# Pair 2's transposes and their copies, emitted with its normalising and ahead of pair 0's products

## The chip, the cores and the metric

The kernel runs on one core of a Trainium2 chip. Times are device microseconds (us) of one execution. A time quoted for a kernel is the median of its runs; every run of this study was of the fast state. Engines are named as in the profile: PE is TensorE, ACT ScalarE, DVE VectorE, POOL GpSimd, and SP the engine whose queue starts the transfers. L311 is line 311 of the kernel.

## The reference, cut to what matters

Four layers work on `x` of 32 batches x 512 tokens x 128 features. Only the first layer matters here:

```python
h = jnp.maximum(_layernorm(x, axis=-1), 0.0)
x = x + _L0_gnn_ref(h, adj, W, e, bias)

def _L0_gnn_ref(input, adj, W, e, bias):
    h0 = jnp.einsum('bnf,fg->bng', input, W[0])
    h1 = jnp.einsum('bnf,fg->bng', input, W[1])
    A = ...                       # softmax over the nonzero entries of adj, 512 x 512
    M = jnp.eye(adj.shape[0])
    out = jnp.einsum('ij,bjg->big', A * M, h0) + jnp.einsum('ij,bjg->big', A * (1.0 - M), h1)
    return out + bias[None, None, :]
```

## The kernel before

The 32 batches are 16 pairs. For each pair ACT normalises eight tiles (`normed`, L216). The result is turned feature-major: on PE for pairs 0 to 2, with ACT copying out of PSUM (L240, L243), and for pairs 3 to 15 by DVE's block transposes and a trip through DRAM (L250, L254, L257). PE then projects it (`p_g`, L357). In the next turn of the loop PE multiplies by the attention matrix: seven products by Strassen's scheme and the diagonal (L311, L654), whose evictions on DVE go through a chain of sums `u`, with GpSimd adding to `x`.

```python
def stats_steps(q, hold=False):
    ...                                   # DVE, L194: bn_stats of x
    yield
    nc.scalar.activation(sd, st[:, :, :, 2], AF.Sqrt, bias=eps, scale=1.0 / D)        # L200
    yield
    nc.vector.reciprocal(rs, sd)                                                     # L203
    nc.vector.scalar_tensor_tensor(sh, st[:, :, :, 1], -1.0, rs, OP.mult, OP.mult)   # L205

def pe_steps(h, name, hT):
    ps = [bank(f"p_{name}_{b}") for b in range(2)]
    for b in range(2):
        for t in range(NT):
            nc.tensor.transpose(ps[b][:, blk(t)], h[:, b, t, :], ident)              # L240
    yield
    for b, p in enumerate(ps):
        nc.scalar.copy(hT[:, :, b, :].rearrange(...), crossed(p))                    # L243

def transposed(h, name):
    for b in range(2):
        nc.vector.transpose(hb[:, :, b]..., h[:, b]...)                              # L250
    ...                                   # SP, L254: four writes to DRAM; L257: one load back
    return hT

def layer0_first(q):
    if q >= 4:
        ln_stats(q)
        yield
    h = normed(q)
    yield
    hT = (transposed_by_pe if q < EARLY else transposed)(h, f"hT0_{q}")              # EARLY = 3
    yield
    if q >= EARLY:
        yield
    for _ in project_steps(q, hT):        # PE L357, then ACT's copies g (L389)
        pass

ORDER = ((1, "a", True), (6, "c", True), (5, "d", True), (7, "c", False), (2, "a", False),
         (4, "c", False), (3, "d", False))

def layer0(q):
    ...                                   # GpSimd: hd (L633), x + bias (L645), right blocks (L282 to L285)
    def evict(k, p):
        if k == 1:
            nc.vector.tensor_add(u[:, 0], pv, spread(b0, 2))                         # L663
            nc.gpsimd.tensor_add(x_of(1, 0), x_of(1, 0), u[:, 0])
        elif k == 6:
            nc.vector.tensor_add(u[:, 1], pv, u[:, 0])                               # L666
            nc.gpsimd.tensor_add(x_of(0, 1), x_of(0, 1), u[:, 1])
        elif k == 5:
            held["d"] = pv
        elif k == 7:
            nc.vector.tensor_add(u[:, 2], pv, u[:, 0])                               # L671
            nc.vector.tensor_add(u[:, 2], held["d"], u[:, 2])                        # L672
            nc.gpsimd.tensor_add(x_of(1, 1), x_of(1, 1), u[:, 2])
        ...                               # k = 2, 4, 3, and the last diagonal: L676, L679, L682, L688
```

`late_sums` makes eight additions of 128x512 on GpSimd for the second layer, one in each turn of the loop from turn 3 on (L275). The schedule puts generators into turns:

```python
waiting = [[layer0(q)] for q in range(NQ)]
next(waiting[0][0])
next(first[2])                            # pair 2's normalising
next(first[3])
next(first[3])                            # pair 3's normalising and block transposes
...
waiting[0] += [first[2], first[4]]
waiting[1] += [first[3], first[5]]
for q in range(6, NQ):
    waiting[q - 4].append(first[q])
waiting[3].append(late_sums())
```

The framework's scheduler then settles each engine's issue order by what it takes to be ready; the source order is a priority only. `keep_in_program_order` and `issue_after` pin an instruction behind another of its engine.

Of the kernel before, what the change touches and what calls it, by code (L numbers as in the profile page):

```python
# [24 lines left out]
def kernel(  # L25
# [345 lines left out]
# [6 lines that stand above are left out]
        hT = (transposed_by_pe if q < EARLY else transposed)(h, f"hT0_{q}")  # L377
# [3 lines that stand above are left out]
        for _ in project_steps(q, hT):  # L381
            pass
# [28 lines left out]
    first = {q: layer0_first(q) for q in range(2, NQ)}  # L411
# [224 lines left out]
    def loads(q):  # L636
        for b in (2 * q, 2 * q + 1):
            tc.keep_in_program_order(load_x(b))
        yield
# [172 lines left out]
    waiting = [[layer0(q)] for q in range(NQ)]  # L812
    next(waiting[0][0])
    next(first[2])
    next(first[3])
    next(first[3])
    for q in range(NQ // 2, NQ):
        waiting[q - NQ // 2].append(loads(q))
    waiting[0] += [first[2], first[4]]
    waiting[1] += [first[3], first[5]]  # L820
    for q in range(6, NQ):
        waiting[q - 4].append(first[q])
    waiting[3].append(late_sums())
# [46 lines left out]
```

## Time and profile before

| | before |
|---|---|
| median of the first 3 runs | 990.46 us |
| profiled run: span, mean granted PE clock | 988.6 us, 0.996 |
| PE busy | 970.4 us, 98% |
| pair 2's projection begins | 60.78 us |
| then each pair takes, in steady state | 9.83 us |

Read it so: PE works without a gap nearly everywhere, so a pair takes its 9.83 us of PE work, 8.04 for the products and 1.79 for a projection. The start of each pair's projection on PE is therefore a ruler: a step longer than 9.83 us is time lost in that pair. The engines' busy time, from the page:

```profile
PE 970.4 (98%) x5918; PEld 805.4 (81%) x5918; DVE 590.4 (60%) x1392; ACT 469.3 (47%) x1063; POOL 399.3 (40%) x526
```

The averages hide stages. This is the windows view of the kernel before (length, then busy us and instructions of PE, PEld, DVE, ACT and POOL; then clock, DMA share, GB/s):

```profile
80.00:90.00 10.00, 10.00 (x92) 10.00 (x91) 8.00 (x24) 4.64 (x12) 9.43 (x12) 1.00 0.58 161
90.00:100.00 10.00, 9.61 (x86) 9.42 (x85) 8.15 (x20) 4.41 (x12) 9.92 (x13) 1.00 0.59 157
```

GpSimd, 40% busy over the kernel, is 99% busy from 90 to 100. PE waits 0.39 us there, and the step from pair 5 to pair 6 is 0.65 us over 9.83. The prediction below does not look at this stretch.

### The profile page before, as it was taken

What the parts mean: (1) busy time and instruction counts of PE and PEld (TensorE: products, weight loads), DVE (VectorE), ACT (ScalarE), POOL (GpSimd) and SP (SyncE); (2) the same over time, 40 slices, a digit from 0 to 9 for tenths busy, and PEclk for the clock granted to TensorE, in tenths of its full rate; (3) what the DMA queues carried; (4) which work ended last, traced back from release to release, by engine and by line L of the source; (5) the groups of instructions that cost most, each with busy time, mean ns of one, the idle gap of its engine ahead of it and who ended that gap; (6) DMA issues with size and microseconds to landing.
All of it is one profiled execution on the core that took longest, in us unless ns stands there. A gap on an engine that the chain in (4) does not pass through costs nothing.

```text
span 988.6 us, 16123 instructions
## 1 busy us (share of the span) xinstructions
PE 970.4 (98%) x5918; PEld 805.4 (81%) x5918; DVE 590.4 (60%) x1392; ACT 469.3 (47%) x1063; POOL 399.3 (40%) x526
## 2 busy tenths in 40 slices
PE   8979999999999999999999999999999999999998
PEld 4679999999999999999977887777767776777776
DVE  8667878656556565566567666665655444444444
ACT  4845455303232232336767654554574554445553
POOL 2559998752134421311243344444133322233322
PEclk9989999999999999999999999999999999999999
DMA  9264544512213122135423343223132121121111
GB/s 257 84 177 129 155 146 109 148 44 60 70 43 86 44 64 65 46 87 145 108 73 115 117 123 106 71 79 87 45 88 77 48 75 54 54 75 44 54 33 43
DMA packets 83023, 87.17 MB, mean 88 GB/s; under 512 B 6784, under 2 KB 73088, under 8 KB 82944
## 3 DMA queue, kind: packets, MB, share of 16 engines
q1 hardware_dynamic: 82944, 86.14, 30.6%
q8 instruction: 47, 0.77, 0.3%
q14 instruction: 32, 0.26, 0.1%
HBM read 44.70 MB, written 41.42 MB: 87 GB/s over the span
## 4 chain that ended last, share of the span: by engine, by line
PE 91%; ACT 1%; DVE 1%; POOL 1%; issue 0%; DVEq 0%; ACTq 0%
PE p_av L780 12%; PE p_l L357 11%; PE p_score L767 11%; PE p_msgT_c L304 4%; PE p_x2T_c L304 4%; PE p_x1T_c L304 4%; PE p_l_c L311 4%; PE p_feat L357 3%; PE p_msgT_d L304 3%; PE p_x1T_a L304 3%; PE p_hv L357 3%; PE p_x2T_d L304 3%; PE p_x2T_a L304 3%; PE p_x1T_d L304 3%; PE p_msgT_a L304 3%; PE p_qkh L754 3%
## 5 line engine op out<-in xcount | busy, mean ns | idle before, releaser
L216 ACT ACTIVATE h<-x,sh,rs 128x128 f32<-128x128 f32 x512 | 208.7, 483 | 70.3 <-PE p_x2T_d L304 46.5
L772 POOL TENSOR_TENSOR ex<-ex,adjTx 128x512 f32<-128x512 f32 x64 | 83.3, 1303 | 197.1 <-issue 147.7
L768 ACT ACTIVATE ex<-p_score 128x512 f32<-128x512 f32 x128 | 71.6, 588 | 122.8 <-issue 113.0
L780 PEld LDWEIGHTS p_av<-qkh_hv,ex 128*128 128x128 f32 x1024 | 118.4, 191 | 9.6 <-issue 7.2
L780 PE MATMUL p_av<-qkh_hv,ex 128*128 128x129 f32 x1024 | 120.3, 275 | 0.9 <-POOL qkh_hv L761 0.6
L767 PE MATMUL p_score<-qkh_hv,hT 128*128 128x512 f32 x256 | 115.2, 593 | 0.0
L250 DVE STREAM_TRANSPOSE hb_hT<-h 128x512 f32<-128x512 f32 x122 | 84.7, 701 | 27.1 <-ACT h L216 26.3
L194 DVE BATCH_NORM_STATS2 bn<-x 128x6 f32<-128x256 f32 x256 | 95.5, 419 | 2.1
L772 DVE TENSOR_TENSOR ex<-ex,adjTx 128x512 f32<-128x512 f32 x64 | 45.9, 717 | 76.2 <-ACT ex L770 76.2
L767 PEld LDWEIGHTS p_score<-qkh_hv,hT 128*128 128x128 f32 x256 | 46.2, 190 | 46.5 <-issue 44.9
L770 ACT ACTIVATE ex<-ex 128x512 f32<-128x512 f32 x128 | 76.6, 631 | 1.8
L282 POOL TENSOR_TENSOR rt_h<-h 128x256 f32<-128x256 f32 x16 | 11.6, 726 | 133.9 <-PE p_x2T_c L304 133.1
L282 POOL TENSOR_TENSOR rt_feat<-feat,feat 128x256 f32<-128x256 f32 x16 | 11.6, 727 | 128.1 <-ACT feat L723 128.1
L389 ACT COPY g<-p_g 128x512 f32<-128x512 f32 x32 | 18.3, 578 | 67.7 <-PE p_g L357 67.5
L357 PE MATMUL p_l<-th,x1T 128*128 128x128 f32 x256 | 49.5, 275 | 0.0
L357 PE MATMUL p_l<-th,x2T 128*128 128x128 f32 x256 | 49.5, 275 | 0.0
L357 PE MATMUL p_l<-th,hs 128*128 128x128 f32 x256 | 49.5, 275 | 0.0
L357 PEld LDWEIGHTS p_hv<-vw,hT 128*128 128x128 f32 x256 | 33.6, 192 | 15.3 <-issue 8.1
L732 POOL TENSOR_TENSOR x<-x,phi2b 128x256 f32<-128x256 f32 x64 | 44.4, 726 | 0.0
L633 POOL TENSOR_TENSOR hd<-hT,adiag 128x512 f32<-128x512 f32 x32 | 40.4, 1273 | 5.6 <-PE p_l_e L654 3.1
L631 POOL COPY hs<-hT 128x512 f32<-128x512 f32 x32 | 19.6, 611 | 54.7 <-PE p_l L357 40.5
L330 ACT COPY x1T<-p_x1T_a 128x256 f32<-128x256 f32 x16 | 6.0, 372 | 74.8 <-PE p_x1T_a L304 74.8
(227 smaller groups left out, 2144.0 us busy)
## 6 DMA issues: line engine op xcount, KB each, us to landing
d_hT<-hb_hT SPq DMA_DIRECT2D x244, 128.0 KB
hT<-d_hT SPq DMA_DIRECT2D x61, 512.0 KB
x<-in_x_dram SPq DMA_DIRECT2D x32, 256.0 KB
out_dram<-x SPq DMA_DIRECT2D x31, 256.0 KB
adj_s<-in_adj_dram SPq DMA_DIRECT2D x4, 256.0 KB
adjT_d<-adjT SPq DMA_DIRECT2D x1, 1024.0 KB
sq<-in_adj_dram SPq DMA_DIRECT2D x4, 256.0 KB
adjTx<-adjT_d SPq DMA_DIRECT2D x4, 256.0 KB
```

The lines of the kernel that those rows point to most:

```text
L194: ins = nc.vector.bn_stats(st[:, k].rearrange("p e s -> p (e s)"), xt[q][:, b, t : t + 2, :].rearrange("p t f -> p f t"))
L216: nc.scalar.activation(h[:, b, t, :], xt[q][:, b, t, :], AF.Relu, bias=shift[q][:, i : i + 1], scale=scale[q][:, i : i + 1])
L250: nc.vector.transpose(hb[:, :, b].rearrange("p j t r -> p t j r"), h[:, b].rearrange("p t (j c) -> p t j c", c=QR))
L304: nc.tensor.matmul(p[:, :H], b[:, k, :], a[:, k, :], start=(first and k == 0), stop=(k == 1), skip_group_check=True)
L357: nc.tensor.matmul(p[:, blk(t)], hT(t), w, start=(i == 0), stop=(i == len(terms) - 1))
L633: nc.gpsimd.tensor_mul(split(s), src, split(scale))
L732: tc.keep_in_program_order(nc.gpsimd.tensor_add(xi, xi, spread(phi2b, 2)))
L767: nc.tensor.matmul(ps, hT[:, t, b, :], qkh, start=True, stop=True)
L768: nc.scalar.activation(ex[:, t, :], ps, AF.Tanh, scale=1.0 / (8.0 * math.sqrt(D)))
L770: nc.scalar.activation(ex[:, t, :], ex[:, t, :], AF.Exp, scale=8.0)
L772: eng.tensor_mul(ex[:, t, :], ex[:, t, :], adjTx[0][:, t, :])
L780: nc.tensor.matmul(po[:, i, : D + 1], ex[:, t, blk(i0 + i)], hv[:, t, :], start=(t == 0), stop=(t == NT - 1))
```

## The change

The intent: PE stood 6.11 us for ACT's copies of pair 2's transposes, which were issued behind pair 4's normalising. Emitting the transposes and the copies early lets the copies run while PE multiplies pair 0.

```diff
     next(waiting[0][0])
     next(first[2])
+    next(first[2])
     next(first[3])
     next(first[3])
 ...
-    waiting[0] += [first[2], first[4]]
-    waiting[1] += [first[3], first[5]]
+    waiting[0].append(first[4])
+    waiting[1] += [first[2], first[3], first[5]]
```

## The prediction

> **What bounds the kernel now.** I read the page first. TensorE (PE) is busy 970.4 of the 988.6 us of the profiled run, and the chain that ended last is 91% PE. So the kernel gets shorter only where PE stands idle, or where PE works slowly, and both are rare. I then asked the list of waits for PE alone, over the whole run; its columns are: who waited for whom, us in total, times, longest.
>
> ```profile
> PE p_g L357 <- ACT hT L243: 6.6, 2, 6.1
> PE p_adjT L395 <- DMA adj_s<-in_adj_dram: 4.2, 2, 3.5
> PE p_msgT_c L304 <- POOL rt_feat L283: 1.4, 1, 1.4
> PE p_l_c L311 <- DVE u_l L666: 1.2, 2, 0.8
> ```
>
> One wait of 6.1 us stands out, and it is the one that the change aims at: PE waits for ScalarE's (ACT) copies of pair 2's transposes out of PSUM before it can project pair 2. The PE rows of the timeline (start, duration) show where it lies, and what comes after it.
>
> ```profile
> 45.60 1.05 PE L311 MATMUL p_l_a<-g,attT 128*128 128x128 f32 x8
> ...
> 53.64 1.04 PE L240 MATMUL p_hT<-ident,h 128*128 128x128 f32 x8
> 60.78 3.78 PE L357 MATMUL p_g<-w,hT 128*128 128x128 f32 x16 [6.11 <-ACT hT L243]
> ```
>
> The chain that ended last, in order of time, has the same work with its share of the path:
>
> ```profile
> 60.78 3.78 PE p_g L357 x16
> 64.56 1.71 PE p_l_a L311 x8
> 66.27 0.90 PE p_l_c L311 x8
> 73.42 1.79 PE p_g L357 x16
> ```
>
> The reader is to see three things. PE runs without a gap from 45.60 to 54.67. It then does nothing until 60.78. And the first work after the gap is slow: 16 matmuls of a projection take 3.78 us there and 1.79 us one pair later; the next eight take 1.71 instead of 0.89 us. The windows view says why: its last three figures are granted PE clock, DMA share and GB/s.
>
> ```profile
> 54.70:60.80 6.10, 0.02 (x1) 0.02 (x1) 4.18 (x15) 4.53 (x13) 1.24 (x2) 0.88 0.72 223
> 60.80:66.10 5.30, 5.30 (x25) 5.30 (x26) 1.68 (x5) 4.51 (x11) 1.43 (x3) 0.50 0.71 195
> 66.10:73.30 7.20, 7.20 (x66) 7.20 (x66) 4.63 (x13) 0.00 (x0) 5.43 (x8) 1.00 0.81 221
> ```
>
> Last, ACT's rows say why the copies are late, though the transposes were done at 54.7:
>
> ```profile
> 46.73 5.10 ACT L216 ACTIVATE h<-x,sh,rs 128x128 f32<-128x128 f32 x13
> 55.23 0.30 ACT L200 ACTIVATE sd<-bn,eps 128x8 f32<-128x8 f32 x1 [3.40 <-DVE bn L194]
> 55.89 0.30 ACT L200 ACTIVATE sd<-bn,eps 128x8 f32<-128x8 f32 x1 [0.35 <-DVE bn L194]
> 56.88 3.19 ACT L216 ACTIVATE h<-x,sh,rs 128x128 f32<-128x128 f32 x8 [0.68 <-DVE sh L205]
> 59.98 0.29 ACT L200 ACTIVATE sd<-bn,eps 128x8 f32<-128x8 f32 x1
> 60.17 1.04 ACT L243 COPY hT<-p_hT 128x512 f32<-128x512 f32 x2
> ```
>
> The two copies stand in ACT's order behind two square roots, pair 4's whole normalising (8 instructions) and a third square root, which wait in turn for VectorE's (DVE) statistics. ACT itself was idle for 3.40 us before that. In the source the copies come before pair 4's normalising; so the issue order is the framework's scheduler's, which orders by what it believes to be ready, and the source order is only a preference. That matters below.
>
> **What the Trainium skill says.** "TensorE: Matmul & The Clock Gate", Part 1: an idle window of about 3.4 us halves PE's clock, and about 3.4 us of sustained work restores it. The trace agrees in kind: after 6.11 us without work the clock is 0.50, and it is back at 1.00 from about 66; here the slow stretch lasts 5.2 us, longer than the page's figure. Part 4 of that page gives a PE transpose about 275 ns in a kernel; the trace has 272 to 273 ns each, and eight in 1.04 us because they overlap. "DVE: scalar operands, raw-bit mode, write accounting and state across instructions", section 5, says that DVE's queue is one in-order queue. I use it for DVE and assume the same of ACT; that the ready copies above waited behind pair 4 agrees.
>
> **The change, part by part.** It adds and removes no instruction. (1) Pair 2's eight transposes and two copies move in the source from behind pair 0's products to just behind pair 2's normalising, ahead of pair 3's normalising and of the products. (2) Pair 2's projection is moved one list later; it still runs in the step after pair 0's products, only behind pair 4's normalising and pair 1's preparation.
>
> What is removed: the idle time of 60.78 - 54.67 = 6.11 us. With the copies issued behind pair 2's normalising (over at about 48.7, from the 13 above at 0.39 us each, of which 5 are pair 2's) they end near 50.5, long before PE's products end. And with no gap the clock stays up. The slow stretch costs now: projection, from its start to the next group's, 64.36 - 60.78 = 3.58 us against 1.79, so 1.79; the next eight matmuls 66.06 - 64.36 = 1.70 against 0.89, so 0.81; the next 0.04. In all 2.64 us. So the most that can be won is 6.11 + 2.64 = 8.75 us, 0.88% of the time. Everything later is PE's chain, with 3.4 us of PE waits from 90 us on, so what is won here reaches the end.
>
> What is moved onto the path: eight transposes, 0.9 us of PE work. They are only displaced, from behind the products to before or among them; no cost by themselves. But they need pair 2's normalised tiles, which ACT delivers one each 0.4 us from 45.5 to 48.7, while PE could start the products at 45.60. If the transposes are strewn among the products as tiles come ready, PE loses some tenths (I take 0.4). If all eight stand ahead of the products, the last waits until about 48.8, products start at 49.0 and not at 45.6 + 0.9 = 46.5: a loss of 2.5. ACT's copies push pair 3's normalising back by 1.04 us; its transposes go through DRAM and are needed about 11 us later than pair 2's, so that is hidden.
>
> **Rivals.** (a) *The wait only moves to DVE.* Pair 1's products need DVE's evictions: the fourth group reads what the second eviction wrote (the 0.8 us wait in the list above). Before the change DVE does pair 4's and pair 5's block transposes ahead of pair 1's first eviction, and those wait for ACT's normalising. PE would now begin pair 2's projection at about 54.7 plus any stall, pair 1's products 1.8 later, and want the second eviction 4.5 after the start, at about 59.2; pair 4's normalising, started 3.1 us after PE's products end as now, delivers its last tile at about 61, DVE's transpose and two evictions make it 62.7. That would be a new wait of 3.5 us, or about 7 if pair 5's stand ahead as well. Against it: one pair later, where no gap exists, the order is the good one:
>
> ```profile
> 76.14 0.42 DVE L663 TENSOR_TENSOR u_l<-p_l_a,b 128x256 f32<-128x256 f32 x1 [0.37 <-PE p_l_a L311]
> 77.03 0.42 DVE L666 TENSOR_TENSOR u_l<-p_l_c,u_l 128x256 f32<-128x256 f32 x1 [0.47 <-PE p_l_c L311]
> 77.48 0.71 DVE L250 STREAM_TRANSPOSE hb_hT<-h 128x512 f32<-128x512 f32 x1
> ```
>
> Without the gap the first step should look like this one. I give rival (a) 0.3; the time would then be 985 to 989.
> (b) *Transposes as a block ahead of the products*: 8.75 - 2.5 = 6.2 won, 984.2. Source order speaks for it; against it speaks that the scheduler goes by readiness (it put an eviction between pair 2's third and fourth tile without a wait). 0.25.
> (c) *The next transfer becomes the wait.* Pair 3's transposed tiles are fetched back from 56.47 on, and would be wanted at about 54.7 + 1.8 + 8.9 = 65.4. That leaves 9 us, less 1 for the delay on ACT: small, 0.05.
> (d) *The whole gain*, with the strewn order: 8.75 less some tenths, about 8: 982.4. The rest of the chance.
>
> **Range and chances.** Weighing 982.4 (0.4), 984.2 (0.25) and 985 to 989 (0.35), I predict 983.3 us, 7.2 less than 990.46. The range 981.4 to 987.8 leaves out the worst of rival (a) below, and above only what 8.75 and a run's spread of 0.4 us allow. 2% would be 19.8 us, over twice what there is to win, and I see no path to a loss of that size: faster by over 2% 0.01, within 2% 0.98, slower by over 2% 0.01.
>
> **What would show each step.** Right: no wait of PE for the copies; clock 1.00 from 45 to 75; the 16 matmuls of pair 2's projection in 1.8 to 1.95 us, beginning within 2 us of 54.7; a DVE order of both evictions before pair 4's block transposes; the end of the span earlier by just what was won by 75 us. Wrong: a wait of PE on the normalised tiles near 46 to 49 (rival b), or on the second eviction near 60 (rival a), or a clock that drops all the same. The prediction would also fail if the scheduler, given another source order, rearranged later layers; then the difference would grow or shrink after 75 us.

## The result, and the profile after

The changed kernel took 986.01 us (985.0 to 986.21, 4 runs), the kernel before 990.09 (988.56 to 990.57, 4 runs, same chip). The ratio is 0.9959, 95% interval 0.9942 to 0.9977: 4.1 us faster, and the same within 2%. A ratio is the mean time of one kernel's fast runs over the mean of the other's of the same rounds, so it is not quite the ratio of the medians. The profiled span fell from 988.6 to 984.4 us, by 4.2.

PE's waits in the changed kernel (who for whom, us in total, times, longest):

```profile
PE p_adjT L395 <- DMA adj_s<-in_adj_dram: 4.4, 2, 3.7
PE p_l_c L311 <- DVE u_l L666: 1.8, 3, 0.8
...
PE p_l_c L311 <- DVE u_l L671: 1.4, 1, 1.4
...
PE p_hT L240 <- ACT h L216: 0.5, 1, 0.5
```

The wait of 6.1 us for the copies is gone. Three small ones are new. The same windows as in the prediction, in the changed kernel:

```profile
54.70:60.80 6.10, 6.10 (x57) 6.10 (x56) 5.97 (x20) 2.38 (x7) 4.29 (x5) 1.00 0.68 189
60.80:66.10 5.30, 5.28 (x48) 5.09 (x47) 4.49 (x11) 3.75 (x11) 4.16 (x7) 1.00 0.78 208
66.10:73.30 7.20, 6.86 (x62) 6.67 (x61) 5.81 (x19) 6.17 (x16) 6.28 (x8) 1.00 0.52 111
```

The window's last three figures are again granted clock, DMA share and GB/s. PE is full where it was empty, and the clock stays at 1.00 where it was 0.50. So both parts of the 8.75 us were removed. The ruler shows where half of it went. Starts of the projections, in us:

| kernel | pair 2 | pair 3 | pair 4 | pair 5 | pair 6 | pair 10 |
|---|---|---|---|---|---|---|
| before | 60.78 | 73.26 | 83.08 | 92.91 | 103.39 | 142.70 |
| after | 56.41 | 66.52 | 76.95 | 88.44 | 99.16 | 138.47 |
| before: step from the pair left of it | | 12.48 | 9.82 | 9.83 | 10.48 | |
| after: step | | 10.11 | 10.43 | 11.49 | 10.72 | |

From pair 6 on the distance between the kernels is constant, 4.2 us, to the end of the span. The book-keeping: 8.75 us to be won, less 0.26 (the first PE work of this stage began at 45.86 after a longer wait at start-up, for 45.60), less 1.48 (from there to pair 2's projection it took 10.55 us, where the kernel before needed 54.67 - 45.60 = 9.07 for the same work), less 0.28, 0.60, 1.66 and 0.24 in the four steps (each against 9.83; the last against 10.48, which the kernel before had itself). That leaves 4.23, the distance at pair 10.

The 1.48 us, in PE's rows of the changed kernel (start, duration):

```profile
45.86 1.10 PE L240 MATMUL p_hT<-ident,h 128*128 128x128 f32 x3
47.49 0.71 PE L240 MATMUL p_hT<-ident,h 128*128 128x128 f32 x2 [0.54 <-ACT h L216]
48.04 0.61 PE L311 MATMUL p_l_a<-g,attT 128*128 128x128 f32 x4
48.49 0.27 PE L240 MATMUL p_hT<-ident,h 128*128 128x128 f32 x1
...
56.41 1.84 PE L357 MATMUL p_g<-w,hT 128*128 128x128 f32 x15
```

Five of the eight transposes stand ahead of the first product. They follow ACT's tiles one by one and take until 48.04, 2.18 us for 0.55 us of work, so 1.63 us are lost; the other three are strewn among the first product's matmuls. (The book-keeping has 1.48, as the 9.07 us of the kernel before run to the modelled end of its last transpose, 54.67; at the transposes' spacing of 0.11 us a next matmul could have started some 0.15 us earlier.) The later steps: these are all of PE's waits between 57 and 101 us that the view names. A start that came 0.19 us late at 61.06 is below what it names.

```profile
71.49 1.16 PE L311 MATMUL p_l_c<-rt_g,attT 128*128 128x128 f32 x8 [0.34 <-DVE u_l L666]
...
85.21 1.16 PE L311 MATMUL p_l_c<-rt_g,attT 128*128 128x128 f32 x8 [1.40 <-DVE u_l L671]
...
93.70 1.16 PE L311 MATMUL p_l_c<-rt_g,attT 128*128 128x128 f32 x8 [0.63 <-DVE u_l L666]
```

And what DVE did ahead of the eviction at 84.77, for which PE waited 1.40 us:

```profile
81.64 0.71 DVE L250 STREAM_TRANSPOSE hb_hT<-h 128x512 f32<-128x512 f32 x1 [0.49 <-ACT h L216]
84.13 0.71 DVE L250 STREAM_TRANSPOSE hb_hT<-h 128x512 f32<-128x512 f32 x1 [1.79 <-ACT h L216]
84.77 0.39 DVE L671 TENSOR_TENSOR u_l<-p_l_c,u_l 128x256 f32<-128x256 f32 x1
```

The block transposes of pair 7 stand ahead of pair 3's third eviction and wait for ACT's tiles. The eviction's own input had been there since about 82.4 (pair 4's projection at 76.95, 1.79 for it and four groups of 0.89 each).

### The profile page after: what moved, and what is told of

Same layout as the page of the kernel before. It is cut to its first block, busy times and chain, and to the rows that moved or that the text cites. A ratio compares the mean times of both kernels' runs of the same rounds, so it can differ in the third digit from the quotient of the medians.

```text
span 984.4 us, 16128 instructions
## 1 busy us (share of the span) xinstructions
PE 969.2 (98%) x5918; PEld 802.8 (82%) x5918; DVE 590.4 (60%) x1392; ACT 469.6 (48%) x1063; POOL 399.4 (41%) x526
## 4 chain that ended last, share of the span: by engine, by line
PE 88%; DVE 2%; ACT 1%; POOL 1%; DMA 0%; issue 0%; DVEq 0%; SPq 0%; ACTq 0%
PE p_av L780 12%; PE p_l L357 11%; PE p_score L767 11%; PE p_msgT_c L304 4%; PE p_x2T_c L304 4%; PE p_x1T_c L304 4%; PE p_l_c L311 3%; PE p_feat L357 3%; PE p_msgT_d L304 3%; PE p_x1T_a L304 3%; PE p_x2T_d L304 3%; PE p_x1T_d L304 3%; PE p_x2T_a L304 3%; PE p_hv L357 3%; PE p_msgT_a L304 3%; PE p_qkh L754 3%
## 5 line engine op out<-in xcount | busy, mean ns | idle before, releaser
L282 POOL TENSOR_TENSOR rt_h<-h 128x256 f32<-128x256 f32 x16 | 11.6, 726 | 133.9 <-PE p_x2T_c L304 133.1
L282 POOL TENSOR_TENSOR rt_feat<-feat,feat 128x256 f32<-128x256 f32 x16 | 11.6, 727 | 128.1 <-ACT feat L723 128.1
```

## The experiments

Twelve runs were made, one of them the changed kernel again, all correct. Each was timed in the rounds of its batch beside the kernel before. I started with two theories. **Theory 1**: PE's later waits come from block transposes that stand ahead of evictions in DVE's queue while ACT has not yet normalised their tiles; put them behind, and the gain grows. **Theory 2**: the other engines set when pair 6 can begin, near 99 us, whatever PE's own order; take one wait away, and another takes its place. The runs' results, with the starts of the projections:

| run | pair 2 | pair 3 | pair 4 | pair 5 | pair 6 | pair 10 | median, us | ratio to before, 95% |
|---|---|---|---|---|---|---|---|---|
| a_again | 55.53 | 65.64 | 76.07 | 87.57 | 98.31 | 137.61 | 985.65 | 0.9960, 0.9947 to 0.9972 |
| a_dve | 57.15 | 67.25 | 80.02 | 91.55 | 101.38 | 143.18 | 990.74 | 1.0008, 1.0002 to 1.0015 |
| a_both | 54.44 | 65.13 | 76.68 | 86.51 | 100.04 | 140.49 | 989.06 | 0.9993, 0.9985 to 1.0002 |
| c_clock | 65.83 | 75.65 | 85.48 | 95.31 | 105.80 | 145.10 | 992.46 | 1.0024, 1.0015 to 1.0033 |
| a_hb7 | 56.37 | 66.48 | 76.90 | 86.73 | 98.79 | 138.10 | 985.93 | 0.9959, 0.9947 to 0.9972 |
| a_mid | 53.80 | 69.17 | 79.00 | 88.83 | 99.32 | 138.63 | 987.85 | 0.9979, 0.9969 to 0.9989 |
| b_pin | 56.31 | 70.40 | 80.22 | 90.05 | 100.52 | 139.82 | 986.52 | 0.9962, 0.9950 to 0.9975 |
| a_block | 57.62 | 67.45 | 77.60 | 89.11 | 99.07 | 138.38 | 988.19 | 0.9974, 0.9963 to 0.9986 |
| a_hb7s | 56.30 | 66.41 | 76.83 | 86.65 | 96.95 | 136.97 | 983.79 | 0.9940, 0.9927 to 0.9952 |
| a_sums | 55.86 | 65.96 | 76.40 | 87.90 | 97.73 | 137.73 | 985.54 | 0.9955, 0.9942 to 0.9967 |
| b_sums | 59.67 | 70.99 | 80.82 | 90.65 | 100.47 | 140.47 | 989.75 | 0.9999, 0.9991 to 1.0008 |
| a_best | 54.77 | 65.47 | 77.56 | 87.38 | 97.21 | 137.21 | 984.95 | 0.9952, 0.9938 to 0.9965 |

The kernel before had medians of 990.05, 989.9, 989.78 and 990.01 us in the four batches.

### a_again: the changed kernel once more

No edit; it is the common base of the first batch.

> The changed kernel once more, so that the other runs of this call can be compared with it on one chip. Both theories: 0.996 of the kernel before, about 986.0 us, pair 2's projection beginning near 56.4 us, pair 6's near 99.2.

Its steps are those of the first run to 0.02 us; only the start differs, by 0.88 us, as PE's first work of this stage began that much earlier. So the steps belong to the kernel, and nearly a microsecond of the position is chance.

### c_clock: the gap filled with unread matmuls

```diff
 # before.py, in pe_steps, behind the transposes, for pair 2 only
+            for i in range(48):
+                nc.tensor.matmul(idle[:, blk(i % NT)], ident, h[:, 1, i % NT, :], start=True, stop=True, ...)
```

> The kernel before, with 48 matmuls that nobody reads issued behind pair 2's transposes, so that PE has work while it waits for the copies. The clock theory: granted clock stays 1.00, pair 2's projection begins near 60.8 us still, takes 1.8 us and not 3.6, and pair 1's first product group 0.9 and not 1.7; 1.2 to 2.6 us faster than before, 987.5 to 989 us (less than 2.6 if VectorE's evictions, which stand behind pair 5's block transposes, are not ready that early). If the slow matmuls there have another cause (the DMA traffic of that stretch), the projection takes 3.6 us still and the time is 990 us.

PE's rows of the run:

```profile
55.11 10.88 PE L244 MATMUL p_idle<-h,ident 128*128 128x128 f32 x96
65.83 1.95 PE L362 MATMUL p_g<-w,hT 128*128 128x128 f32 x16
```

The filler was nearly twice as long as the gap: 48 float32 matmuls are 96 records of some 0.11 us. So pair 2 began 5.05 us later than in the kernel before, and the run is slower as a whole. What it was made for it shows: with PE kept busy the 16 matmuls of pair 2's projection take their normal time, and the step to pair 3 is 9.82 us, not 12.48. The slow clock was worth 2.66 us in the profile of the kernel before; the prediction had 2.64. The rival on record, DMA traffic, falls too: from 60.8 to 66.1 the DMA share of this run is 0.84 (239 GB/s), more than the 0.71 (195 GB/s) of the kernel before, and the clock there is 1.00 with matmuls at their normal pace. The time, 992.46, is what neither side had expected, because of the filler's length.

### a_dve and a_both: block transposes of pairs 4 to 7 all pinned late

```diff
 # after.py, in transposed, for pairs 4 to 7
-            nc.vector.transpose(hb[...], h[...])
+            tc.keep_in_program_order(nc.vector.transpose(hb[...], h[...]))
 # in layer0: pair q + 3's step is taken behind the fourth product of pair q
-        for _ in products(...): pass
+        for n, _ in enumerate(products(...)):
+            if 1 <= q < 5 and n == 3: next(first[q + 3])
```

a_both also puts pair 2's transposes behind the fourth product group of pair 0, and the copies ahead of the next square root on ACT.

> The changed kernel with VectorE's block transposes of pairs 4 to 7 pinned behind the first four evictions of pairs 1 to 4. Theory 1 (PE's later waits come from block transposes that stand ahead of evictions in VectorE's order and wait for ScalarE): the waits of PE on VectorE from 58 to 99 us, 0.3 + 0.6 + 1.7 + 0.9 us longer than the steady 9.83 us per pair, mostly vanish; pairs follow each other each 9.83 us from pair 3 on; 982.6 to 983.5 us. Theory 2 (the other engines' work sets when pair 6 can start, whatever PE's order): pair 6's projection still begins near 99 us and the time stays at 985.5 to 986.5 us.

> As a_dve, and pair 2's transposes pinned behind the fourth of pair 0's product groups, by when its normalised tiles are all there; the copies come ahead of the square roots on ScalarE. Theory 1: the 1.6 us that PE lost at the head vanish too, pair 2's projection begins near 54.8 us, 981 to 982 us. Theory 2: no more than a_dve, 985.5 to 986.5 us.

Both numbers of both theories missed. SP's queue of a_dve, and the wait that it made on PE:

```profile
66.12 9.12 SPq L256 DMA_DIRECT2D d_hT<-hb_hT  x5
75.47 0.34 SPq L259 DMA_DIRECT2D hT<-d_hT  x1
```

```profile
80.02 2.43 PE L359 MATMUL p_g<-w,hT 128*128 128x128 f32 x16 [2.78 <-DMA hT<-d_hT]
```

Pair 4's load back from DRAM stands in SP's queue behind five writes. The fifth is pair 5's, and pair 5's block transposes had been pinned to 73.61. So pair 4 waited for pair 5's transposes after all, through another queue. The next step, 11.53 us, has no wait of PE at all: the clock was 0.50 from 81.5 to 84.9 (windows view), and half of these 3.4 us is the 1.70 by which the step is too long. These two runs therefore say nothing against Theory 1; they say that the pins were too many. They also put the prediction's rival (c) in its place: in the changed kernel pair 4's load was issued at 71.42. With the 4.55 us that a_dve's load took from issue to PE's start, it would be there near 76.0, an estimate, and pair 4 began at 76.95. It was not the wait, but only 1 us from it.

a_both's head agrees that the 1.48 us are due to the transposes' place: pair 2 began at 54.44. Later on, PE waits 0.60, 1.46 and 0.46 us for DVE's second evictions, and at pair 6 2.82 us for a transfer, as in a_dve. Before the 1.46, DVE had stood 2.31 us for one of GpSimd's additions to x (at 67.71).

### a_mid: transposes among the products, copies early, DVE left to the scheduler

```diff
 # after.py: the second next(first[2]) is taken out, and in layer0(0)
+            if n == 3: next(first[2])     # transposes pinned behind the fourth product on PE,
+                                          # the copies ahead of the next square root on ACT
```

> The changed kernel, with pair 2's eight transposes pinned behind the fourth product group of pair 0 on TensorE and their copies put ahead of the next square root on ScalarE: it keeps the early copies and takes away TensorE's lock-step with ScalarE's normalising. The program's issue order on VectorE comes out differently: halves of the block transposes of pairs 4 to 7 stand before every second eviction of pairs 1 to 3. Theory 1: the head of the changed kernel is 0.7 to 1.6 us shorter (pair 2's projection begins at about 54.8, where the changed kernel had 55.5 and 56.4), but the steps from pair 2 to pair 6 lose more than in the changed kernel, at least 3 us together; time 985.5 to 987.5. Theory 2: pair 6 begins near 99 here too, and the time is 985.7.

Pair 2 began at 53.80, the earliest of all runs. Then PE's rows show the worst step of all:

```profile
57.38 1.06 PE L317 MATMUL p_l_d<-rt_g,sums_att 128*128 128x128 f32 x8
62.28 2.08 PE L317 MATMUL p_l_c<-rt_g,attT 128*128 128x128 f32 x8 [3.85 <-DVE u_l L672]
```

This is the prediction's rival (a), where the prediction put it and nearly of its size (3.5 us): in this order DVE does both halves of pair 4's block transposes before pair 1's second eviction. (L672 of this run is the L666 of the changed kernel.) PE stood 3.85 us, and its clock fell again (0.50 from 61.9 to 65.3, by the windows view); the two together are nearly all of the 5.54 us that the step is too long. The step took 15.37 us. After it PE is so late that nothing else holds it until pair 5, so that pair 6 at 99.32 is no point for Theory 2. The loss in the steps, over 3 us, is as Theory 1 had it; the time, 987.85, is above both theories' numbers. The changed kernel escapes this only because the scheduler set both evictions first there.

### b_pin: the copies alone moved

```diff
 # before.py, in stats_steps
-        nc.scalar.activation(sd, ..., AF.Sqrt, ...)
+        ins = nc.scalar.activation(sd, ..., AF.Sqrt, ...)
+        if q == 4 and q not in early: tc.keep_in_program_order(ins)      # behind pair 2's copies
```

> The kernel before, with only ScalarE's part of the change: its square root for pair 4 is pinned behind pair 2's copies, so the copies stand where the changed kernel has them in ScalarE's queue, while TensorE's transposes stay behind pair 0's products. TensorE should wait about 1.9 us for the copies in place of 6.11 and keep its full clock, so pair 2's projection begins at about 57 and its step to pair 3 is about 10. VectorE's order is the one of the a_mid run. Theory 1: the steps from pair 2 to pair 6 lose at least 3 us together, as there, so the time is 986.5 to 989. Theory 2: pair 6 begins near 99, and the time is 985.7.

PE's rows:

```profile
56.31 2.05 PE L359 MATMUL p_g<-w,hT 128*128 128x128 f32 x16 [1.41 <-ACT hT L245]
...
61.51 0.49 PE L313 MATMUL p_l_a<-g,attT 128*128 128x128 f32 x2 [0.47 <-DVE u_l L665]
63.53 1.71 PE L313 MATMUL p_l_c<-rt_g,attT 128*128 128x128 f32 x8 [1.53 <-DVE u_l L668]
```

With PE's order untouched up to pair 2's projection and only ACT's copies early, the wait for them is 1.41 us, not 6.11, and pair 2 begins as early as in the changed kernel. So the ACT part of the change does the work, and the early transposes on PE are not needed for it. DVE then has the same bad order as in a_mid, and the next step takes 14.09 us, 4.26 too many. Not all of this is DVE: by the windows view the clock is 0.51 from 63.9 to 67.4, after PE waits of only 0.47 and 1.53 us, and half clock for some 3.4 us costs about 1.7 us. The time, 986.52, is at the lower edge of Theory 1's range and above Theory 2's number. Its runs fall into two groups (985.4 to 985.9 with a recorded clock of 1.0, 987.1 to 987.6 with 0.998); the profile is from the slower group. The stretch at half clock is probably what parts them: 3.4 us at half clock lower the mean over 986 us to 0.998 and cost 1.7 us, and the groups' medians lie 1.84 us apart.

### a_block: all eight transposes ahead of the first product

```diff
 # after.py: each of hT0_2's transposes, and pair 0's first product, by keep_in_program_order
```

> The changed kernel, with all eight of pair 2's transposes pinned ahead of pair 0's first product, so that TensorE stands for ScalarE's normalising. The prediction priced this at 2.5 us where the changed kernel showed 1.6 (first product to pair 2's projection against the kernel before). Theory 1: pair 2 begins 0.9 to 1.8 us later than in the changed kernel's two traces (56.4 and 55.5), near 57.3, the later steps are as in the changed kernel (VectorE's order is the same around the evictions), and the time is 986.5 (0.9964). Theory 2: pair 6 begins at the same 98.3 to 99.2, and the time is 985.7.

```profile
47.88 1.86 PE L240 MATMUL p_hT<-ident,h 128*128 128x128 f32 x5 [0.54 <-ACT h L216]
49.58 1.06 PE L315 MATMUL p_l_a<-g,attT 128*128 128x128 f32 x8
```

From the first transpose (46.25) to the first product it took 3.33 us, of which 0.89 is work: a loss of 2.44, as the prediction's rival (b) had it (2.5). But pair 6 begins at 99.07, where the changed kernel had 99.16. The head was 1.2 us worse than in the first run of the changed kernel, and nothing came of it by pair 6: the steps to pairs 3, 4 and 6 were shorter in turn, by 0.28, 0.28 and 0.76 us. That is Theory 2. The medians do not agree with the profile here: three runs are at 985.8 to 986.2 us (the profiled one among them), four at 988.2 to 988.8 with a clock of 0.998. No profile shows the slower group, but 0.998 is what one stretch at half clock of 3.4 us would leave, as in b_pin. That would explain some 1.7 of the 2.65 us between the groups' medians; this is an estimate.

### a_hb7: only pair 7's block transposes moved

```diff
 # after.py, in transposed, for pair 7
+        with tc.issue_after(evicted[name]):            # L672 of pair 3
             nc.vector.transpose(hb[...], h[...])
```

> The changed kernel, with one thing undone on VectorE alone: the two halves of pair 7's block transposes stand behind the third eviction (lines 671 and 672) of pair 3's products, not ahead of it. In the changed kernel VectorE stood 1.79 us at the second half, waiting for ScalarE's normalising, and TensorE then waited 1.40 us for the eviction behind it; the step from pair 4's projection to pair 5's took 11.49 us. Theory 1 (PE's later waits come from block transposes that stand ahead of evictions in VectorE's queue): the 1.40 us wait is gone, that step is about 10.0, and the kernel takes about 1.4 to 1.6 us less than the changed one, 984.1 (0.9940 of the kernel before). Theory 2 (the other engines set when pair 6 can begin, near 99 us, whatever stands first): pair 5 begins earlier, but pair 6 still begins at 98.3 to 99.2 after a new wait, and the time stays at 985.7 (0.9956).

The scheduler also set some of DVE's statistics and one addition to x on GpSimd otherwise. Both theories wrote down what happened first: the wait of 1.40 us is gone, and the step to pair 5 is 9.83 us. Theory 1's time did not come. Pair 6 began at 98.79, and the step to it took 12.06 us in place of 10.72. PE's, DVE's and then GpSimd's rows of this run (seven to nine lines were added above: its L691 is L682 of the changed kernel, its L674 is L667, and its L282 is the L275 of `late_sums`):

```profile
93.16 1.16 PE L318 MATMUL p_l_c<-rt_g,attT 128*128 128x128 f32 x8 [1.80 <-DVE u_l L673]
```

```profile
88.41 0.43 DVE L691 TENSOR_TENSOR x<-p_l_d,x 128x256 f32<-128x256 f32 x1 [1.17 <-POOL x L674]
```

```profile
86.42 1.28 POOL L282 TENSOR_TENSOR adj_s<-adj_s 128x512 f32<-128x512 f32 x1
87.64 0.74 POOL L674 TENSOR_TENSOR x<-x,u_l 128x256 f32<-128x256 f32 x1
```

DVE waited for an addition to x that stood behind an addition of `late_sums`, and PE then waited for DVE. So Theory 2 was right here, and it now had a suspect: GpSimd. I called that **Theory 3**, with the rival **Theory 4** that DVE's own block transposes and statistics of pairs 8 and 9 hold pair 6.

### a_hb7s, a_sums and b_sums: late_sums three turns later

```diff
-    waiting[3].append(late_sums())
+    waiting[6].append(late_sums())
```

This one line was changed in a_hb7, in the changed kernel and in the kernel before. The issue orders of PE, ACT and DVE in the traces are the same, only GpSimd's differs. (The text on record calls the line 282 of the changed kernel; it is 275 there, and 282 in a_hb7.)

> The a_hb7 run, with GpSimd's eight additions of late_sums (line 282 of the changed kernel, 1.28 us each, 10.2 us together) begun three turns of the loop later (turn 6 for turn 3); the issue orders of TensorE, VectorE and ScalarE are the same, only GpSimd's differs. In a_hb7 pair 5 began 1.71 us earlier than in the changed kernel, and pair 6 only 0.37 earlier: GpSimd was 9.92 us busy of the 10 between 90 and 100, and VectorE waited 0.61, 1.17 and 0.26 us for its additions to x. Theory 3 (GpSimd with late_sums on it sets when pair 6 begins): the step from pair 5 to pair 6 is 9.83 to 10.1 in place of 12.06, pair 6 begins at 96.6 to 97.1, and the time is 1.7 to 2.2 us under a_hb7's, near 984.0 (0.9940). Theory 4 (VectorE's block transposes and statistics of pairs 8 and 9 set it, whatever GpSimd does): pair 6 still begins at 98.3 to 99.2, and the time stays at 985.7 to 985.9.

> The changed kernel with late_sums begun three turns later and nothing else; issue orders of TensorE, VectorE and ScalarE are the changed kernel's. Theory 3: the wait for pair 7's block transposes stays (the step from pair 4 to pair 5 is still near 11.5), the step to pair 6 falls from 10.72 to about 9.9, and the time is 0.6 to 0.9 us under the changed kernel's, near 984.9 (0.9949). Theory 4: both steps and the time are the changed kernel's (985.7 to 986.0).

> The kernel before with late_sums begun three turns later and nothing else. There the step from pair 5 to pair 6 was 10.48 in place of 9.83. Theory 3: it becomes 9.83, and the time is 0.65 us less, 989.3 to 989.5 (0.9993). Theory 4: the step stays at 10.48 and the time is that of the kernel before (990.0).

The step from pair 5 to pair 6 went from 12.06 to 10.30 us in a_hb7s, from 10.72 to 9.83 in a_sums, from 10.48 to 9.82 in b_sums. By the steps Theory 3 holds and Theory 4 falls, though a_hb7s kept 0.2 us more than the 10.1 at most that was expected. By the time only a_hb7s is where Theory 3 had it. The windows view of a_hb7 and then of a_hb7s, same columns as above:

```profile
90.00:100.00 10.00, 8.20 (x72) 7.91 (x71) 8.32 (x23) 4.23 (x12) 9.92 (x13) 1.00 0.45 122
```

```profile
90.00:100.00 10.00, 9.96 (x88) 9.68 (x87) 8.26 (x26) 4.99 (x13) 8.31 (x12) 1.00 0.58 169
```

But much of the loss was only moved. In all three the step from pair 8 to pair 9 is now 10.5 us, where `late_sums` now stands. How GpSimd holds DVE up shows in two tiny instructions, `sh` of 128x8. First DVE and GpSimd of the changed kernel, before the wait of 0.63 us at 93.70:

```profile
90.95 1.83 DVE L205 SCALAR_TENSOR_TENSOR sh<-bn,rs 128x8 f32<-128x8 f32 x2
```

```profile
89.04 1.26 POOL L275 TENSOR_TENSOR sums_adj<-sums_adj,adj_s 128x512 f32<-128x512 f32 x1
90.27 2.49 POOL L633 TENSOR_TENSOR hd<-hT,adiag 128x512 f32<-128x512 f32 x2
```

Then DVE of a_sums, at the same place and where `late_sums` has gone:

```profile
90.19 0.29 DVE L205 SCALAR_TENSOR_TENSOR sh<-bn,rs 128x8 f32<-128x8 f32 x2
...
119.66 1.86 DVE L205 SCALAR_TENSOR_TENSOR sh<-bn,rs 128x8 f32<-128x8 f32 x2
```

The two instructions end at 92.78, and GpSimd's second `hd` at 92.76. With GpSimd idle they take 0.29 us, with GpSimd at work 1.83 to 1.86. "SBUF — State Buffer" of the Trainium skill, in "SBUF: two separate sides", says why: a DVE operation with two SBUF inputs and a GpSimd operation that reads SBUF take the same pair of ports, whole instructions at a time, and the other one blocks. `sh` reads `bn` and `rs`, both in SBUF. The evictions read one input from PSUM and keep their 0.4 us. The trace agrees wherever I looked: every single `sh` of the changed kernel between 45 and 80 us that took over 0.2 us ended within 0.04 us of the GpSimd instruction that ran when it began. It is the two extra additions of `late_sums` just before (86.44 and 89.04, 1.27 and 1.26 us) that push `hd` under `sh`.

In time: a_hb7s has the lowest median of the study, 983.79 us, 6.0 under the kernel before. Against a_hb7 the traces differ by 1.13 us at pair 10, the medians by 2.1. a_hb7's runs scatter (984.65 to 987.58): two of the five, 985.95 and 987.58, have a mean clock of 0.998, and all of a_hb7s have 1.0. The median of the other three is 984.83, 1.04 above a_hb7s's, close to the 1.13 of the traces. a_sums moved by 0.1 to 0.5 us against the changed kernel's two medians, less than the 0.6 to 0.9 expected and within the runs' spread, as the new loss of 0.70 us at pair 9 takes most of the 0.89 won. b_sums gained nothing (0.9999), for the same reason: 0.66 won at pair 6, 0.68 lost at pair 9. (Its profile is of its fastest execution, 988.18; the table's starts before pair 6 are early by luck of the start and of the clock, not by the edit.)

### a_best: everything together

```diff
 # a_mid, with DVE pinned by issue_after:
+  pair 4's block transposes behind L666 and L672 of pair 1; pair 5's behind L688 of pair 1;
+  pair 6's behind L688 of pair 2; pair 7's behind L672 of pair 3; late_sums in turn 6
```

> Everything the runs have shown, put together: the changed kernel with pair 2's transposes behind the fourth product group of pair 0 and their copies ahead of the next square root (as a_mid), VectorE's block transposes queued where the a_hb7s run had them (pair 4's behind the second and third evictions of pair 1, pair 5's and 6's behind the last evictions of pairs 1 and 2, pair 7's behind the third of pair 3), and late_sums begun three turns later. Theory 3 (the parts add up): the head ends 1.5 us or more earlier than in a_hb7s (pair 2 begins at 54 to 54.8), the steps from pair 2 to pair 6 are those of a_hb7s (10.1, 10.4, 9.8, 10.3), pair 6 begins near 95.2, and the time is 1.0 to 1.7 us under a_hb7s's, about 982.3 (0.9925). Rival (pair 4's transfer becomes the wait: in a_hb7s its load was issued at 71.4, behind two writes of pair 5, and would land near 76.0, where pair 4 began at 76.83): TensorE waits for it before pair 4's projection, pair 6 begins near 96.3, and the time is 983.3 to 983.8.

The head was as hoped: pair 2 began at 54.77, 1.53 us before a_hb7s. At pair 10 it is 0.24 us behind it. DVE's and PE's rows where the lead went:

```profile
68.05 0.42 DVE L708 TENSOR_TENSOR x<-p_l_e,x 128x256 f32<-128x256 f32 x1 [2.06 <-POOL x L690]
```

```profile
72.09 1.16 PE L326 MATMUL p_l_c<-rt_g,attT 128*128 128x128 f32 x8 [1.99 <-DVE u_l L683]
```

DVE's last eviction of pair 1 waits 2.06 us for GpSimd's addition, pair 5's block transposes come behind it, and PE waits 1.99 us for the eviction after those. The rival on record, pair 4's transfer, was not it: PE had no wait for a transfer. The parts do not add up, because PE cannot get further ahead of GpSimd, DVE and ACT than they let it. The time, 984.95 (983.71 to 986.52), is not better than a_hb7s's, and outside what either side had expected.

## Why the prediction was right or wrong, point by point

The class was right and the time, 986.01, is inside the range of 981.4 to 987.8. The point was 983.3: a gain of 7.2 where 4.1 came. The prediction's own weights give 984.5 (0.4 x 982.4 + 0.25 x 984.2 + 0.35 x 987), not 983.3. And the range held in part by luck: 986.01 lies in the band of 985 to 989 that was kept for rival (a), a wait at pair 1's second eviction, and the loss came elsewhere.

- **What can be won, 8.75 us: right.** The wait of 6.11 us is gone (windows after). The clock's 2.64 us were confirmed by c_clock's 2.66. They are the figure of one profile, though: in b_sums the same gap of 6.11 us was followed by a step of 11.32 us, so the slow clock cost 1.49 there. The stretch at half clock is some 6.8 us long in both (59.3 to 66.2 and 55.8 to 62.6, windows view), but began 4.65 us into the gap in the one and 2.2 us in the other, so more of it fell where PE was idle anyway.
- **Clock, place and order: right.** The clock stayed at 1.00, pair 2's projection began 1.74 us after 54.67, and DVE did both of pair 1's first evictions before pair 4's block transposes.
- **Transposes strewn 0.4 us, as a block 2.5: the case was neither.** Five stood ahead and three were strewn, and it cost 1.48. As a block it cost 2.44 (a_block), so that size held. Wholly strewn was not run.
- **Rival (a), a wait on DVE of 3.5 us: the mechanism was right.** (The reason given was off: the fourth group does not read what the second eviction wrote. It adds to the PSUM bank "c" that this eviction must have read first, by `ORDER` and `products`. And the 0.8 us wait that was pointed to lies at 205 us.) In the order that the prediction feared it is 3.85 us (a_mid). The changed kernel has the other order at pair 1, but the same thing at pair 3 (1.40 us), which the prediction did not look for.
- **The step that failed: "Everything later is PE's chain ... so what is won here reaches the end".** The evidence offered was 3.4 us of PE waits from 90 us on, in the kernel before. That says how little PE waited when it was late, not how early it may come. The lead was 6.74 us at pair 3, 6.13 at pair 4 and 4.23 at pair 6, so it was not settled by 75 us as the prediction's own check demanded. Once PE came early it met the other engines: 0.28, 0.60, 1.66 and 0.24 us were given back in four steps, 2.78 us in all, sized at nothing by the prediction. Behind the largest stood block transposes that waited for ACT (a_hb7 removed it); behind the last, GpSimd (a_sums: the step is 9.83, the kernel before's own 0.65 gone as well). And they stand in for one another: with the first removed (a_hb7), 1.34 of its 1.66 us came back in the step behind it.
- **"One pair later ... the order is the good one"**: one pair was too few to look at. The windows of the kernel before had GpSimd at 9.92 of 10 us only 13 us behind the rows shown.
- **Rival (c), the transfer, 0.05: right for the changed kernel.** (Its sum has 8.9 us for pair 1's products, which take 8.04.) It was closer than thought: by the estimate above, pair 4's load was there about 1 us before it was used.

Left open: what the slower group of runs in a_block does beyond a likely stretch at half clock; and which share of the 0.28 and 0.60 us is DVE's order and which the engines' work, since the runs that moved pair 4's and 5's transposes (a_dve, a_both) changed SP's order as well. The trace of the changed kernel shows this much: DVE was busy 3.90 us of the four from 57 to 61, with an `sh` of 0.57 us at 59.24 under GpSimd's work, and 4.40 of the 4.50 from 66.5 to 71. Unlike at pair 3, no wait for ACT stands ahead of these two evictions.

## What to carry to other kernels

Before you count a removed wait as gain, ask how early each other engine could have its next results ready, stage by stage, and not only at the average: an engine that is 40% busy over the kernel can be the bound for the 10 us of one pair. A gain at the head of a pipeline is kept only as far as the slowest of the others lets the fast one lead; look at the start of each iteration, before and after, to see where the lead stops growing. And where a queue is in order, what waits for a far input must not stand ahead of what the critical engine wants: in a_hb7 moving it behind one eviction removed a wait of 1.4 us (most of which came back a step later, at GpSimd), and in a_dve moving too many of them made one of 2.8 through another queue.

## What the Trainium skill lacked or had wrong

- "SBUF — State Buffer", "SBUF: two separate sides", states the lock between DVE and GpSimd, and the runs agree. It gives no time for a tiny DVE instruction, where the rule shows most: two `sh` of 128x8 took 0.29 us without GpSimd and 1.83 to 1.86 us with it, six times as long.
- "TensorE: Matmul & The Clock Gate", Part 1, has the clock halved after an idle window of about 3.4 us. Here shorter gaps did it: one of 2.78 us in a_dve (0.50 from 81.5 to 84.9), and two of 0.47 and 1.53 us, half a microsecond apart, in b_pin (0.51 from 63.9 to 67.4). A gap of 2.82 us in a_both did not (1.00 from 100 to 103). That equal gaps of 6.11 us cost 2.65 us in the kernel before and 1.49 in b_sums fits the page's statement that the window runs freely.
- No page has the price of making one engine earlier against several in-order queues: of 8.75 us removed from PE's path, 4.23 were kept.
